# Attention with a spectral feed-forward on one core: the last unit finished 128 rows at a time, the spectral weights folded, loads and a small chain reordered

## The chip, the core and the metric

The kernel runs on one core of a Trainium2 chip. A core has a matrix engine (TensorE, PE in the profile, with PEld for its weight loads), a vector engine (VectorE, DVE), a scalar engine (ScalarE, ACT), GpSimd (POOL), and SyncE (SP), which here only starts transfers. Each engine takes its own instructions strictly in the order in which they were written and waits for others by semaphores; transfers (DMA) are started from the queues of SP, ACT and POOL. Matrix products land in the PSUM memory; everything else lies in SBUF. The metric is the device time of one execution in microseconds (us).

## The reference

The input x is 2 sequences of 2048 rows of 256 numbers, all float32.

```python
xn = layernorm(x)                       # over the 256 columns
q = rope((xn @ wq).reshape(B, S, 16, 16))
k = rope((xn @ wk).reshape(B, S, 4, 16)); v = (xn @ wv).reshape(B, S, 4, 16)
# head i of q uses head i % 4 of k and v
scores = einsum('bshd,bthd->bhst', q, k) / sqrt(16), causal
attn = softmax(scores) @ v, reshaped to (B, S, 256), @ wo
w = complex(w_freq_real, w_freq_imag)   # 256 x 256
ffn = real(ifft(fft(xn) @ w)) + bias    # over the columns
out = x + attn + ffn
```

Since the spectral part is linear in xn, it is one 256 x 256 real matrix (`mff`), made once: inverse-transform table times weights times transform table, with the cosine table `dc` and the sine table `ds` as inputs. The rest is `xn @ mff`.

## The kernel before, in words

**Blocks, units, steps.** The rows are cut into 8 blocks of 512: block n is sequence n % 2, part j = n // 2 of 4. A unit is a block and one of 4 groups of 4 heads; there are 32, in the order of the blocks. A unit takes 4(j+1) steps t, one for each 128 keys, so the first two blocks have 4 steps per unit and the last two 16. The last four steps of a unit lie on the causal diagonal: of the block's 512 columns only those from `lo` on are worked on (512, 384, 256, 128 columns).

**Preparing a block** (`chain`, `project`). `load_x` brings the 512 rows (L170). `row_stats` takes mean and variance of four 128-row pieces on DVE (L237, L238); `row_power` makes the reciprocal root on POOL (L243, L244); `row_shift` makes minus mean times it on DVE (L249); `norm` applies both to the four pieces (L399; DVE for block 0, POOL for the others). PE transposes the block (`transpose_x`, L411), ACT copies it out (`xnT`, L414), and `features` multiplies it with the ordered projection weights `wp` in three parts, K and V together, Q0 and Q1 (tile `ps_q`, products of the helper at L155); ACT copies each out (L427). `rotate` and `split` apply the rotary table and cut each float32 into three bfloat16 parts (seven elementwise passes for each of the three parts, L518 to L556, DVE for block 0 and POOL for the others). SP's queue then stacks the parts into the operands `kst` and `qst` (L393; for most units over a detour through DRAM, `run`).

**A unit.** `maxima` computes rows by keys on PE (tile `sm`, L155, L627, L631) and their maxima on DVE (L636); the negated maxima go through PE, ACT and a transfer (`spread`, L671 to L678) into `qst`, so that `scores` (tiles `st`, then `sp` once all maxima are done; L155, L734, L738) comes out shifted. ACT takes the exponential (L745, L747) and on the diagonal POOL zeroes the upper triangle (`affine_select`, L752). `values` multiplies with the values and a column of ones into `av` (L780), which over all steps of the unit is one accumulation; `take` copies it to SBUF on ACT (L791). For most units the sums of the ones column are divided out over a DRAM detour from POOL's queue (`put` to `scale`). The last two units go another way: `divide` transposes `avs` on PE (tile `ps_a`, L850), divides on DVE (L854, L855), and `turn_back` transposes the result back (tile `ps_t`, L865) for ACT to copy (L869). `output` multiplies with `mff` and `wo_sb` (tile `po`) and adds the residual on DVE (L906); a transfer of 256 rows writes two pieces out (L914). For the last block three of the four terms of `output` are done ahead.

**The spectral matrix** (`spectral_matrix`, once). ACT negates the sine table (L320). Four pieces `left` (tile `ps_ff`) make the two 256 x 256 halves `at_` and `et_` from real and imaginary weights, each as 8 products of 128 x 128 by 128 x 256; two pieces `right` (tile `ps_mff`) make `mff` from them with 8 more each. A `product` is four matmul instructions of 32 columns of weights; on float32 each shows as two entries in the profile, so that a group of 16 matmul entries is two products. The inputs are loaded by six transfers on POOL's queue (`load_late`, L225 to L228).

**What sets the order.** The text of the kernel is a planner: `clock` holds an estimated time for each engine, `there` when a thing will be ready, `use` and `send` advance them by a duration written in the code (0.53 us for `row_stats`, for example). A loop picks the next piece for PE among row maxima (A), scores (B), values (V), spreads (S) and the queues of other pieces (`streams`, each with a step from which it may and one by which it should be done), and emits pieces of the other engines as their estimated start comes up. Each engine then runs in the emitted order. A changed cost or a changed piece therefore shifts the order of all later work. At the start, 48 transposes of the identity (L968) keep PE busy until data is there. PSUM gives three banks to `st`, shared by all small pieces, two pairs to `sm`/`sp` and one to `av`.

Of the kernel before, what the change touches and what calls it, by code (L numbers as in the profile page):

```python
# [23 lines left out]
def tile_attn_plus_spectral_ffn(  # L24
# [141 lines left out]
    def load_x(n):  # L166
        send("sp", 512, [slot("xt")], [("xt", "in", n)])
        take_slot("xt")
        xt[n] = work.tile([P, NI, D], F32, tag="xt", bufs=2, name=f"xt{n}")
        nc.sync.dma_start(out=xt[n], in_=block_rows(n))  # L170
# [46 lines left out]
    def load_late():  # L217

        for name, src, tag, bufs in (
# [6 lines left out]
            send("pool", 256, (), ["spec"])  # L226
        nc.gpsimd.dma_start(out=wo_sb, in_=wo.rearrange("(c p) n -> p c n", p=P))
# [5 lines left out]
    def row_stats(n, i):  # L233
# [5 lines left out]
        use("dve", 0.53, [("xt", "in", n)], [("mv", n)])  # L239
# [7 lines left out]
    def row_shift(n):  # L247
        shift[n] = work.tile([P, NI], F32, tag="sh", bufs=2, name=f"sh{n}")
        nc.vector.scalar_tensor_tensor(  # L249
            shift[n], mv[n][:, :, 0], -1.0, rstd[n], ALU.mult, ALU.mult  # L250
        )
        use("dve", 0.2, [("rs", n)], [("sh", n)])
# [23 lines left out]
    def rotary_table(j):  # L276
        ex = []

        def expand():
# [17 lines left out]
            use("dve", 1.15, at, [("trx", j)])  # L297
# [14 lines left out]

    mff = const.tile([P, NK, D], F32, name="mff")

    def spectral_matrix():
        wre, wim, dc, ds_ = (spec[k] for k in ("wre", "wim", "dc", "ds"))
        neg_s = work.tile([P, NK, D], F32, tag="xr", bufs=3, name="neg_s")
        at_ = work.tile([P, NK, D], F32, tag="xr", bufs=3, name="at_")
        et_ = work.tile([P, NK, D], F32, tag="xr", bufs=3, name="et_")
        nc.scalar.mul(neg_s, ds_, -1.0)  # L320
        use("act", 0.48, ["spec"], ["neg_s"])
# [3 lines left out]
        pieces = []  # L325

        def left(o, name, dst, parts):
            cols = slice(o * P, (o + 1) * P)
            ps = bank(f"ps_ff{o}")[:, :D]
            for a, (w, f) in enumerate(parts):  # L330
                for c in range(NK):
                    product(
                        ps, w[:, c, cols], f[:, c, :],
                        start=(a == 0 and c == 0), stop=(a == 1 and c == NK - 1),
                    )
            nc.scalar.mul(dst[:, o, :], ps, 1.0 / D)
            through_bank(1.87, ["neg_s"], "act", 0.29, [("left", o, name)])

        def right(r):
            cols = slice(r * P, (r + 1) * P)  # L340
            ps = bank(f"ps_mff{r}")[:, :D]
            for a, (w, f) in enumerate(((at_, dc), (et_, neg_s))):
                for c in range(NK):
                    product(
                        ps, w[:, c, cols], f[:, c, :],
                        start=(a == 0 and c == 0), stop=(a == 1 and c == NK - 1),
                    )
            nc.scalar.copy(mff[:, r, :], ps)
            lefts = [("left", o, name) for o in range(NK) for name in ("at", "et")]
            through_bank(1.87, lefts, "act", 0.29, [("mff", r)])  # L350
            if r == NK - 1:
                for tag, k in (
                    ("inv", 0), ("inv", 1), ("attT", 0), ("avs", 0),
# [3 lines left out]

        for o in range(NK):
            pieces.append((["neg_s"], lambda o=o: left(o, "at", at_, ((wre, dc), (wim, ds_)))))
            pieces.append((["neg_s"], lambda o=o: left(o, "et", et_, ((wim, dc), (wre, neg_s)))))  # L360
        lefts = [("left", o, name) for o in range(NK) for name in ("at", "et")]
        for r in range(NK):
            pieces.append((lefts, lambda r=r: right(r)))
        return pieces
# [14 lines left out]
    def project(n):  # L379
# [5 lines left out]
        raw, sw, swp, part, ra, at = {}, {}, {}, {}, {}, {}  # L385
# [710 lines left out]
    while True:  # L1096
# [88 lines left out]
        elif kind == "V":  # L1185
# [3 lines left out]
            if first[u + 1] == v_next:  # L1189
                take(u)  # L1190
# [64 lines left out]
```

## Time and profile before

| | us |
|---|---|
| median of 4 runs | 923.95 (923.50 to 924.41) |
| the profiled execution, its own time | 924.41 |
| its span in the trace | 922.7 |
| PE busy in the span | 902.9 |
| DVE busy | 748.3 |
| ACT busy | 653.9 |
| POOL busy | 371.0 |

The profiled execution is the slowest of the four runs; 1.7 us of its time lie outside the span. Busy time is the union of an engine's instructions. Lines Lnnn are those of the kernel before. In a group or a timeline, `out<-in` names the tiles, `xN` counts instructions, and the remark in brackets tells how long the engine had been idle before and what it waited for.

### The profile page before, as it was taken

What the parts mean: (1) busy time and instruction counts of PE and PEld (TensorE: products, weight loads), DVE (VectorE), ACT (ScalarE), POOL (GpSimd) and SP (SyncE); (2) the same over time, 40 slices, a digit from 0 to 9 for tenths busy, and PEclk for the clock granted to TensorE, in tenths of its full rate; (3) what the DMA queues carried; (4) which work ended last, traced back from release to release, by engine and by line L of the source; (5) the groups of instructions that cost most, each with busy time, mean ns of one, the idle gap of its engine ahead of it and who ended that gap; (6) DMA issues with size and microseconds to landing.
All of it is one profiled execution on the core that took longest, in us unless ns stands there. A gap on an engine that the chain in (4) does not pass through costs nothing.

```text
span 922.7 us, 38985 instructions
## 1 busy us (share of the span) xinstructions
PE 902.9 (98%) x17324; PEld 498.7 (54%) x17324; DVE 748.3 (81%) x1056; ACT 653.9 (71%) x1375; POOL 371.0 (40%) x556
## 2 busy tenths in 40 slices
PE   7999899999999999999999999999999999999997
PEld 4666565555555555555554555555455554645443
DVE  6878887789789996998995999979789988798601
ACT  3266666588657884888866778857687877588784
POOL 7298766835662424822336420302572021102111
PEclk9999999999999999999999999999999999999999
DMA  5435823340244011340002600010143001100000
GB/s 166 119 89 140 211 91 107 112 116 31 75 124 112 27 38 38 107 129 26 15 26 85 152 27 13 27 60 14 34 111 84 14 3 38 49 14 16 25 1 24
DMA packets 41992, 62.13 MB, mean 67 GB/s; under 512 B 8840, under 2 KB 32120, under 8 KB 41824
## 3 DMA queue, kind: packets, MB, share of 16 engines
q1 hardware_dynamic: 32400, 41.18, 16.6%
q0 software_dynamic: 8128, 17.69, 5.8%
q8 instruction: 135, 2.21, 1.0%
q10 hardware_dynamic: 1296, 0.79, 0.3%
q14 instruction: 33, 0.27, 0.1%
HBM read 32.75 MB, written 18.40 MB: 55 GB/s over the span
## 4 chain that ended last, share of the span: by engine, by line
PE 90%; DVE 5%; ACT 3%; issue 1%; DMA 1%; ACTq 0%; POOL 0%; DVEq 0%; POOLq 0%
PE av L780 24%; PE st L155 22%; PE sm L155 17%; PE sm L631 7%; PE po L155 6%; PE ps_q L155 4%; DVE mx L636 2%; PE sm L627 2%; PE sp L155 2%; PE st L738 2%; ACT es L745 1%; PE ps_x L411 1%; ACT es L747 1%; PE st L734 1%; PE ps_m L671 0%
## 5 line engine op out<-in xcount | busy, mean ns | idle before, releaser
L636 DVE TENSOR_REDUCE mx<-sm 128x2 f32<-128x1024 f32 (+3 forms) x640 | 649.2, 1058 | 85.4 <-PE sm L631 41.5
L745 ACT ACTIVATE es<-st 128x512 f32<-128x512 f32 (+3 forms) x1194 | 552.3, 541 | 177.1 <-PE st L155 146.2
L155 PE MATMUL st<-qst,kst 115*32 115x512 bf16 (+3 forms) x4264 | 327.0, 354 | 1.1 <-ACT es L745 0.4
L780 PE MATMUL av<-es,va 128*32 128x512 f32 (+3 forms) x2560 | 299.9, 529 | 0.6 <-issue 0.3
L155 PE MATMUL sm<-kst,qst 112*32 112x512 bf16 x3072 | 239.5, 379 | 0.8 <-issue 0.7
L155 PEld LDWEIGHTS <-kst 115*32 115x32 bf16 x4608 | 160.9, 95 | 140.6 <-issue 65.0
L752 POOL TENSOR_SCALAR_AFFINE_SELECT es<-es 128x256 f32<-128x256 f32 x192 | 77.1, 409 | 273.7 <-ACT es L745 232.5
L155 PEld LDWEIGHTS <-qst 112*32 112x32 bf16 x3072 | 95.9, 96 | 94.3 <-issue 65.5
L631 PE MATMUL sm<-kst,qst 112*32 112x32 bf16 (+15 forms) x2048 | 121.1, 279 | 0.7 <-DMA qst<-part 0.7
L780 PEld LDWEIGHTS av<-es,va 128*32 128x32 f32 x2560 | 85.3, 109 | 28.5 <-issue 2.4
L627 PE MATMUL sm<-mask,ident_h 128*32 128x64 bf16 (+3 forms) x2048 | 99.4, 200 | 1.1 <-DVE mx L636 0.9
L631 PEld LDWEIGHTS <-qst 112*32 112x32 bf16 x2048 | 65.5, 97 | 34.0 <-issue 20.6
L627 PEld LDWEIGHTS <-ident_h 128*32 128x32 bf16 x2048 | 65.3, 95 | 32.1 <-issue 25.0
L906 DVE TENSOR_TENSOR xr<-po,xr 128x256 f32<-128x256 f32 x36 | 15.3, 424 | 51.5 <-PE po L155 49.5
L803 POOL DMA_DIRECT2D res<-avs x30 | 18.2, 608 | 77.1 <-ACT avs L791 75.0
L155 PE MATMUL ps_q<-xnT,wp 128*32 128x512 f32 x384 | 45.2, 599 | 0.0
L747 ACT ACTIVATE es<-sp 128x1024 f32<-128x1024 f32 (+3 forms) x43 | 36.6, 907 | 7.6 <-PE sp L155 7.4
L427 ACT COPY raw<-ps_q 128x512 f32<-128x512 f32 x24 | 14.1, 586 | 34.8 <-PE ps_q L155 34.8
L518 POOL TENSOR_TENSOR ra<-raw,cs 128x512 f32<-128x512 f32 (+1 forms) x21 | 27.3, 1301 | 24.2 <-ACT raw L427 23.0
L738 PE MATMUL st<-qst,kst 115*32 115x480 bf16 (+15 forms) x512 | 36.3, 279 | 0.6 <-issue 0.6
L155 PE MATMUL po<-wo_sb,attT 128*32 128x256 f32 x512 | 34.4, 379 | 0.7 <-ACT attT L869 0.7
L155 PE MATMUL po<-mff,xnT 128*32 128x256 f32 x512 | 34.4, 380 | 0.0
(108 smaller groups left out, 656.7 us busy)
## 6 DMA issues: line engine op xcount, KB each, us to landing
qst<-run SPq DMA_DIRECT2D x62, 128.0 KB
res<-avs POOLq DMA_DIRECT2D x30, 256.0 KB, 3.1
run<-part SPq DMA_DIRECT2D x31, 192.0 KB
qst<-run SPq DMA_DIRECT2D x31, 192.0 KB
xt<-in_L_attn_x_dram SPq DMA_DIRECT2D x8, 512.0 KB
xr<-in_L_attn_x_dram SPq DMA_DIRECT2D x16, 256.0 KB
out_dram<-xr SPq DMA_DIRECT2D x16, 256.0 KB
sw<-raw SPq DMA_DIRECT2D x60, 64.0 KB
```

The source lines that it names most:

```text
L155: nc.tensor.matmul(to[q : q + QD], lhsT[:, q : q + QD], rhs, start=start, stop=stop)
L518: e.tensor_tensor(ra[c][:r], raw[c][:r], cs[j][:r, 0, :], ALU.mult)
L627: nc.tensor.matmul(to[:, at:wd], ident_h[:, q : q + QD], mask[:, q:], start=True, stop=True, skip_group_check=True,)
L631: nc.tensor.matmul(to[:, : at + QD], rows[:, q : q + QD], keys[:, : at + QD], start=False, stop=True, skip_group_check=True,)
L636: nc.vector.tensor_reduce(t["mx"][:, i, 2 * pr : 2 * pr + 2, k], ps[0][:, :, :wd], AX.X, ALU.max)
L738: nc.tensor.matmul(to[:, at:], keys[:, q : q + QD], rows[:, at:], start=False, stop=True, skip_group_check=True,)
L745: nc.scalar.activation(es[u, t, pr][:, e, lo:], ps[:, lo:], AF.Exp, scale=SCALE)
L747: nc.scalar.activation(es[u, t, pr][:, :, lo:], wide[pr][:, :, lo:], AF.Exp, scale=SCALE)
L752: nc.gpsimd.affine_select(out=es[u, t, pr][:, :, lo : lo + P], in_=es[u, t, pr][:, :, lo : lo + P], pattern=[[0, 2], [1, P]], compare_op=A ...
L780: nc.tensor.matmul(av[u][QD * h : QD * (h + 1), lo:], va[at_block[b, t // NI]][:, t % NI, h, :], es[u, t, h // 2][:, h % 2, lo:], start=(t ...
L803: nc.gpsimd.dma_start(out=res[n, c][f], in_=avs[u])
L906: nc.vector.tensor_tensor(xr[n, r][:, e, :], po, xr[n, r][:, e, :], ALU.add)
```

## The change

- **Last unit by 128 rows.** For the very last unit, each diagonal step of `values` closes the 128 columns that need no later keys. `take_part` copies those 128 columns alone, `divide_part` and `turn_back` work on 128 rows, the last term of `output` for a piece needs only its own rows, and the last block's rows go out in four transfers of 128 rows in place of two of 256.
- **Spectral weights folded.** Cosine and sine are even and odd under k to 256 - k. Six small GpSimd instructions add and subtract mirrored columns of the weights into `vc` and `vs`; then one half `left` is needed in place of two, and `right` needs one product per 128 columns of contraction in place of two. The pieces on PE are `left(o, 0)`, `left(o, 1)` for o = 0, 1 and `right(0)`, `right(1)`. A further table `half_sb` is loaded by two transfers on POOL's queue, into one of the eight `es` slots. The negation on ACT is gone.
- **Projections in two pieces.** `features(c, k)` is planned for each half of the contraction, the first as soon as the first half of `xnT` is there; other work may come between them.
- **First loads and table.** Block 0 is loaded by four transfers of 128 rows; statistics of a piece wait for its own piece. The first rotary table's expansion on DVE stands before `row_shift(0)`, not after it.
- **Negative shift on GpSimd.** For blocks 1 to 7 `row_shift` is two POOL instructions in place of one on DVE.
- **Planner costs.** `row_stats` 0.6 for 0.53, the table 1.6 for 1.15.

```diff
 def load_x(n):
-        send("sp", 512, [slot("xt")], [("xt", "in", n)])
+        at = slot("xt")
         take_slot("xt")
...
-        nc.sync.dma_start(out=xt[n], in_=block_rows(n))
+        step = NI if n else 1
+        for i in range(0, NI, step):
+            send("sp", 128 * step, [at], [("xt", "in", n, k) for k in range(i, i + step)])
+            nc.sync.dma_start(out=xt[n][:, i : i + step, :], in_=block_rows(n)[:, i : i + step, :])
...
+        half_sb = spec["half"] = work.tile([P, D], F32, tag="es", bufs=ES, name="half_sb")
+        nc.gpsimd.dma_start(out=half_sb[0:1], in_=dft[0, P : P + 1, :])
+        nc.gpsimd.dma_start(out=half_sb[1:P], in_=dft[1, 1:P, :])
...
     def row_shift(n):
+        if n == 0:
             nc.vector.scalar_tensor_tensor(
                 shift[n], mv[n][:, :, 0], -1.0, rstd[n], ALU.mult, ALU.mult
             )
+        else:
+            nc.gpsimd.tensor_scalar(shift[n], mv[n][:, :, 0], -1.0, None, ALU.mult)
+            nc.gpsimd.tensor_tensor(shift[n], shift[n], rstd[n], ALU.mult)
+            use("pool", 0.4, [("rs", n)], [("sh", n)])
...
-            use("dve", 1.15, at, [("trx", j)])
+            use("dve", 1.6, at, [("trx", j)])
...
+        fold(of_c, up, wre[:, :, up], wre[:, :, down], ALU.add)
+        fold(of_s, up, wim[:, :, up], wim[:, :, down], ALU.add)
+        fold(of_c, far, wim[:, :, down], wim[:, :, up], ALU.subtract)
+        fold(of_s, far, wre[:, :, up], wre[:, :, down], ALU.subtract, True)
+
+        def left(o, a):
+            v, f = ((of_c, dc), (of_s, ds_))[a]
+            if a == 0:
+                held[o] = bank(f"ps_ff{o}")[:, :D], take_slot("st")
+            ps, k = held[o]
+            for c in range(NK):
+                product(
+                    ps, v[:, c, o * P : (o + 1) * P], f[:, c, :],
+                    start=(a == 0 and c == 0), stop=(a == 1 and c == NK - 1),
+                )
...
-            for a, (w, f) in enumerate(((at_, dc), (et_, neg_s))):
-                for c in range(NK):
-                    product(
-                        ps, w[:, c, cols], f[:, c, :],
-                        start=(a == 0 and c == 0), stop=(a == 1 and c == NK - 1),
-                    )
+            for c, f in enumerate((dc[:, 0, :], half_sb)):
+                product(
+                    ps, left_sb[:, c, r * P : (r + 1) * P], f,
+                    start=(c == 0), stop=(c == NK - 1),
+                )
...
-        def features(c):
+        def features(c, k):
+            if k == 0:
+                held[c] = bank(f"ps_q{n}_{c}"), take_slot("st")
+            ps, at_st = held[c]
+            product(ps, wp[:, k, c, :], xnT[n][:, k, :], start=(k == 0), stop=(k == NK - 1))
...
+        if last and t >= j * NI:
+            take_part(u, t - j * NI)
+    def take_part(u, i):
...
+        cols = slice(i * P, (i + 1) * P)
+        nc.scalar.copy(avs[u][:, cols], av[u][:, cols])
+    def divide_part(u, i):
...
+        nc.tensor.transpose(ps, avs[u][:, i * P : (i + 1) * P], ident)
+        nc.vector.reciprocal(rc, heads[:, :, DH])
+        nc.vector.tensor_tensor(
+            att[n][:, i, g - 2], heads[:, :, 0:DH],
+            rc.unsqueeze(2).to_broadcast([P, NKV, DH]), ALU.mult,
+        )
+    def turn_back(n, c, i):
+        ps = bank(f"ps_t{n}_{c}_{i}")[:, 0:P]
+        nc.tensor.transpose(ps, att[n][:, i].rearrange("p g h e -> p (g h e)"), ident)
+        nc.scalar.copy(attT[n][:, c, i * P : (i + 1) * P], ps)
...
+        if terms[-1] == 2 * NK - 1 and n == NB - 1:
+            nc.sync.dma_start(out=out[b, at : at + P, :], in_=xr[n, r][:, e, :])
...
     row_power(0)
     load_late()
+    table_0 = rotary_table(0)
+    table_0[0]()
     row_shift(0)
```

## The prediction

> **What bounds the kernel now.** I read the engines' busy times first, then PE in stretches of the span, then the chain at both ends.
>
> ```profile
> PE 902.9 (98%) x17324; PEld 498.7 (54%) x17324; DVE 748.3 (81%) x1056; ACT 653.9 (71%) x1375; POOL 371.0 (40%) x556
> ...
> 10.00:15.00 5.00, 4.59 (x24) 2.73 (x28) 4.43 (x16) 2.25 (x4) 4.94 (x9) 0.66 0.75 247
> ...
> 100.00:120.00 20.00, 16.80 (x533) 11.84 (x529) 15.45 (x28) 13.96 (x38) 15.52 (x23) 1.00 0.74 194
> 120.00:140.00 20.00, 19.88 (x532) 14.45 (x528) 19.10 (x36) 9.77 (x28) 12.07 (x20) 1.00 0.27 87
> ...
> 220.00:230.00 10.00, 9.37 (x199) 5.51 (x197) 9.79 (x21) 6.85 (x18) 7.77 (x15) 1.00 0.02 5
> ...
> 910.00:915.00 5.00, 3.92 (x60) 1.79 (x53) 0.26 (x1) 2.44 (x5) 2.01 (x5) 1.00 0.00 0
> 915.00:920.00 5.00, 2.59 (x36) 1.35 (x36) 2.12 (x5) 0.59 (x1) 0.00 (x0) 1.00 0.13 43
> ```
>
> A stretch's columns are its length, the busy time of PE, PEld, DVE, ACT and POOL, PE's granted clock, the transfers' share and GB/s. PE is busy for all but 19.8 us. By the same view these lie so: 5.6 up to 34 us, 4.5 from 34 to 140 (3.2 of them in the row from 100 to 120), 2.9 from 140 to 880, 0.6 to 900, 6.2 after 910. So work taken from PE counts in full in the middle; at the start and the end the chain counts.
>
> The start, as the timeline shows it (start, length, engine, line):
>
> ```profile
> 7.83 1.05 POOL L244 TENSOR_TENSOR rs<-rs,neg_half 128x4 f32<-128x4 f32 x1
> 8.92 0.16 DVE L249 SCALAR_TENSOR_TENSOR sh<-mv,rs 128x4 f32<-128x4 f32 x1 [1.51 <-POOL rs L244]
> 9.00 1.63 DVE L293 TENSOR_REDUCE trx<-trig 128x128 f32<-128x128 f32 x8
> 10.54 1.90 DVE L399 TENSOR_SCALAR xt<-xt,rs,sh 128x256 f32<-128x256 f32 x4
> ...
> 26.05 1.05 PE L155 MATMUL ps_ff<-dc,wim 128*32 128x256 f32 x16
> 26.91 1.05 PE L155 MATMUL ps_ff<-neg_s,wre 128*32 128x256 f32 x16
> ...
> 33.08 0.23 POOL L243 TENSOR_SCALAR rs<-mv 128x4 f32<-128x4 f32 x1 [10.16 <-DVE mv L238]
> ```
>
> DVE stands 1.51 us before the shift and expands the table only then; two groups of spectral products start 0.86 us apart; POOL idles 10.16 us. The end, by the chain of waits:
>
> ```profile
> 913.39 0.59 ACT avs L791
> 914.03 0.67 PE ps_a L850 x4
> 914.72 0.27 DVE rc L854
> 915.01 0.43 DVE att L855
> 915.49 0.67 PE ps_t L865 x4
> 916.18 0.59 ACT attT L869
> 916.82 0.68 PE po L155 x8
> 918.83 0.42 DVE xr L906
> ```
>
> After the last `values` (913.37) seven links in a row take 5.9 us; the last two writes take the remaining 3.45.
>
> **Spectral products.** Before: four `left` and two `right`, 12 groups at 0.86 us, 10.3 us of PE. After: 12 products, 6 groups, 5.2 us. PE does 5.2 us less. The negation on ACT (0.63 us) and two copies (0.385 each) go, all beside other work: nothing.
>
> **Folds.** Four POOL instructions of 128 x 254 and two of 128 x 4. No row shows a mirrored read. From below, POOL's 128x256 select, 0.41; from above, a whole 128x512 float32 subtraction, 1.17. I take half of that, 0.6, since the four 128x256 norms take 0.55 each: 2.6 us with the two small ones (range 1.8 to 5).
>
> **First loads.** SP issues four transfers (0.44 to 0.5 us each), so the table's issue moves from 1.30 to about 2.8 and block 1's from 1.83 to 3.3. The whole block landed at 5.16; its last quarter, issued at 2.3, should do so at about 5.1. DVE is in its memsets until 4.64, then takes 2.14 us of statistics without a wait: done 6.8, not 7.32. The table expands there (6.8 to 8.45) while POOL makes the root (1.4 us, as now). If the table lands late, the shift queued behind it waits too; all early loads were over by 7.6, so that costs at most 0.8. Norms begin at 8.7, not 10.54. PE's first transposes follow its warm-up (ended 8.36) at once, where it now idles 1.9 us.
>
> The two-piece projection lets K's first half start after the first copy (11.5) and the second follow the next copy. Its last product ends at about 13.2, against 16.2.
>
> **The clock.** The granted clock was 1.00 in the windows up to 11 us and 0.50 from 12 to 14, after PE's gap from 8.36 to 10.30; the eight transposes took 2.32 us against 1.02 later, K's projection 2.38 against 1.9. I put that loss at 1.8 us. The first gap goes, but a new one comes, next paragraph. I take 1.7 us lost again; ends 0 and 3.4.
>
> **What PE waits for next.** In the emitted order, PE after block 0's last swap product comes to block 1's transposes, K projection and half a `left` before unit 0's first row maximum; the seven other spectral groups that filled this time before are gone or later. Block 1's norms hang on POOL's queue: root 8.3; eight transfer issues (six took 4.45 us, so 5.7 with the two of `half_sb`) to 14.0; ones for block 2 and 1 (2.5 each) to 19.0; root 1.4; ones again 2.6, to 23.1; shift 0.4 (0.24 and 0.15, the rows of L243 and L249); norms 2.2 to 26.1; folds to 28.8. PE is through with block 0 at about 21.8. It then idles about 4 us, does 3.6 us of work and reaches the row maxima at 29.6, or 31.5 at half clock. Their operand landed at 31.8; DVE's chain in front starts 2.9 us earlier, so it is there at 28.9. Idle PE time up to there: 1.4, 0.8 among the norms, three waits for copies at 0.7, 3.9, in all 8.2 for 5.6: plus 2.6.
>
> The Trainium skill speaks against the change here ("TensorE: Matmul & The Clock Gate", Part 1): about 3.4 us of idling put PE at half clock until a busy window has passed. This trace lost the clock after a gap of 1.9 us for about 3.4 us. By the page the new gap costs up to 1.7 us, and without it the sum would be 1.7 better.
>
> **Early stalls.** POOL's rotation of block 1 began at 44.32 and, with block 2's, kept it almost without a pause to 106. Block 1's root and shift had waited for DVE's queue until 33; in the new order both precede, and POOL's rotation starts right after the folds, near 30. So stacks for blocks 1 and 2 come some ten us sooner, and the stalls from 70 to 120, where few scores were left to do while block 2 was made, have less cause. POOL has 2.6 of folds, 1.2 of issues and 0.4 per block more, and DVE is 19.10 of 20 busy in the next stretch. I take 2.0 of the 4.5 us; ends minus 4.0 and plus 2.
>
> **Shift in the middle.** Once (226.09) DVE stood 1.13 us in L249 against 0.15 otherwise, in a stretch where DVE is full and PE idles 0.63. I take 0.5 (0 to 1). Elsewhere POOL's second small instruction replaces a handover.
>
> **The tail.** Scores and the last selects come as before, but two copies of 128 columns (0.28, as the 128x128 exponential) stand before the last exponentials on ACT: plus 0.6. PE meets each part's chain in between; its order has the last `values` after two transposes and an output term: plus 0.2. So the last `values` ends at 914.1. Then, by 128 columns: copy 0.28, transpose 0.27, division 0.3 (a quarter of the columns of L854 and L855, 0.26 and 0.42), two residuals and an output term on the same queues 0.9, transpose 0.27, copy 0.28, output 0.45, residual 0.42: 3.1 us, to 917.2, against 919.25. Four issues at 0.62 on SP fit, and the last write carries 128 KB where two of 256 KB overlapped: 0.5 less. Tail: minus 2.6 (1.0 to 3.3).
>
> **Planner.** Everything later is reordered a little; from 140 to 880 PE idles 2.9 us. I take zero, ends plus and minus 1.5.
>
> **Sum.** -5.2 + 2.6 + 0 (clock, 1.7 for 1.8) - 2.0 - 0.5 - 2.6 + 0 = -7.7, so 924.4 becomes 916.7. The profiled execution is 0.45 above the median; against the median I say 916.3.
>
> **The rivals.**
> - R1, the early stalls stay (DVE at 19.1 of 20 sets them, not POOL) and the clock costs 1.7 more: -7.7 + 2.0 + 1.7 = -4.0, 920. For it: DVE's stretch after 120.
> - R2, the stalls all but go and the new gap is 2 us shorter, POOL's queue being through sooner than I sum it: -9.7 with one of these, -11.7 with both, 914.2 or 912.3; I say 913. For it: POOL's long pause before 44.
> - R3, slower: POOL becomes the bound before 120 us. The folds and issues stand in front of block 1's rotation; if mirrored reads are slow or its projection comes late, block 2's operands land 7 us after today's and PE idles that much more: -5.2 + 2.6 - 0.5 - 2.6 + 7 = +1.3, 925. It decides from a delay of 6 us on. Against it: POOL would need to lose the 14 us by which its rotation starts earlier, and that again.
> - R4, the trimmed products only open waits (the new gap, the tail's interleaving): within 0.2%, 923.5.
>
> **Chances and range.** Forecast 0.50 (914.8 to 918.5), R1 0.20, R2 0.18, R3 0.07, R4 0.05. 0.2% (1.85 us) is about what a measurement tells apart. Faster (below 922.1): the first three but for 0.01, 0.87; same R4, 0.05; slower R3 and that 0.01, 0.08. The range reaches over R2 and R1: 911.5 to 921.5.
>
> **What would show it.** Six spectral groups at 0.86; norms at 8.7, K's product over by 13.3; a PE gap near 22 to 26 with a clock below 1.00 after it; row maxima at 29 to 32; POOL's rotation near 30; under 3 us idle from 34 to 140; the last residual ending 4.3 us after the last exponential, where it is 6.9 now (912.34 to 919.25). Wrong it would be if folds took over 1.2 us each, if PE idled more than now from 34 to 140, or if PE's busy time fell by less than 4.

## The result, and the profile after

The changed kernel takes 927.89 us (median of 52 runs), the kernel before 926.17 us (79 runs, measured beside it and beside the experiments): a ratio of 1.002, with a 95% interval from 1.0013 to 1.0028. It is 0.2% slower. The forecast was 916.3 us with a range from 911.5 to 921.5, 0.8% faster than the 923.95 us then known; it was wrong, in size and in sign. The profiled execution of the changed kernel took 927.19 us, 2.8 more than the one of before, with a span of 925.4 us for 922.7.

The engines' busy times of the changed kernel:

```profile
PE 902.1 (97%) x17228; PEld 494.7 (53%) x17228; DVE 750.0 (81%) x1055; ACT 653.3 (71%) x1378; POOL 381.6 (41%) x578
```

Six groups of spectral products are gone from PE, 5.2 us, but its busy time fell by only 0.8, and its idle time grew by 3.5. The same view by stretches as in the prediction (length, busy time of PE, PEld, DVE, ACT, POOL, PE's granted clock, transfers):

```profile
20.00:25.00 5.00, 2.30 (x20) 0.29 (x12) 4.72 (x9) 0.59 (x1) 4.73 (x8) 0.93 0.31 103
25.00:30.00 5.00, 2.80 (x12) 1.59 (x16) 4.83 (x6) 0.60 (x2) 4.95 (x9) 0.50 0.37 96
30.00:34.00 4.00, 4.00 (x24) 1.07 (x28) 1.63 (x7) 0.94 (x2) 1.99 (x3) 0.50 0.79 212
...
100.00:120.00 20.00, 17.22 (x552) 11.91 (x552) 15.81 (x32) 12.93 (x35) 18.13 (x25) 1.00 0.78 202
120.00:140.00 20.00, 18.66 (x503) 11.54 (x496) 17.81 (x32) 11.75 (x33) 10.50 (x18) 1.00 0.26 80
220.00:230.00 10.00, 9.80 (x204) 5.31 (x196) 9.56 (x24) 8.78 (x20) 5.92 (x12) 1.00 0.14 47
```

PE now idles 8.1 us up to 34 us (5.6 before), 6.2 from 34 to 140 (4.5 before) and 2.6 from 140 to 880 (2.9 before). And from 25 to 34 us it works at half its clock, which makes the work there longer: 1.7 us on block 1's first projection, 1.7 on block 1's transposes (2.74 us for the 1.06 of block 0's) and 0.6 on a spectral group. Another 1.4 us of the busy time are the warm-up at the start, which took 8.30 us in this execution and 6.94 in that of before. That is where most of the 5.2 us went, and more.

The start, as the timeline shows it (start, length, engine, line; lines are those of the changed kernel, in which the norm is L436, the shift L264, a fold L347, the last split pass L595, the row maximum on DVE L676). Below, "the first scores" are unit 0's first products of `maxima` on PE (tile `sm`), and "the first row maximum" is what DVE makes of them:

```profile
7.31 1.64 DVE L307 TENSOR_REDUCE trx<-trig 128x128 f32<-128x128 f32 x8 [0.41 <-DMA trig<-rope_dram]
8.87 0.15 DVE L259 SCALAR_TENSOR_TENSOR sh<-mv,rs 128x4 f32<-128x4 f32 x1
9.05 1.46 DVE L436 TENSOR_SCALAR xt<-xt,rs,sh 128x256 f32<-128x256 f32 x4
...
25.38 3.19 POOL L436 TENSOR_SCALAR xt<-xt,rs,sh 128x256 f32<-128x256 f32 x4
25.98 0.47 PE L448 MATMUL ps_x<-ident,xt 128*128 128x128 f32 x1 [2.98 <-POOL xt L436]
28.88 1.24 DVE L595 TENSOR_TENSOR part<-rb,part 128x512 bf16<-128x512 f32 x1
29.88 3.64 PE L155 MATMUL ps_q<-xnT,wp 128*32 128x512 f32 x16
31.27 0.72 POOL L347 TENSOR_TENSOR vs<-wre 128x254 f32<-128x254 f32 x1
33.30 1.68 PE L155 MATMUL ps_ff<-dc,vc 128*32 128x256 f32 x16
35.21 0.76 DVE L676 TENSOR_REDUCE mx<-sm 128x2 f32<-128x256 f32 x2 [3.47 <-PE sm L671]
```

The opening itself came nearly as told: norms at 9.05, not 10.54 (8.7 told), and block 0's first projection over at 13.72, not 16.1 (13.2 told). But the reader can follow how the lead is lost. PE is done with block 0 at 23.0 and stands 2.98 us before block 1's first transpose, until POOL has normed a piece. It comes out of that gap at half clock, so the projection takes 3.64 us (1.9 at full clock) and a spectral group 1.68 (1.05). DVE has block 0's last split at 30.12, but the first scores stand behind all this on PE's queue. DVE's first row maximum starts at 35.21; before, it was 32.83.

The end, by the chain of waits:

```profile
917.11 0.36 PE av L822 x8
917.46 0.43 PE po L155 x8
917.89 0.28 PE ps_a L919
918.18 0.12 PE ps_t L931
...
918.32 0.28 ACT attT L932
...
919.90 0.68 PE po L155 x8
...
920.60 0.42 DVE xr L971
```

From the last `values` to the last residual it takes 3.55 us (5.9 before), but the last `values` comes 1.9 us after the last exponential (915.58) where it was 1.0 before: on PE it stands behind the transposes and output terms of the other parts.

### The profile page after: what moved, and what is told of

Same layout as the page of the kernel before. It is cut to its first block, busy times and chain, and to the rows that moved or that the text cites. A ratio compares the mean times of both kernels' runs of the same rounds, so it can differ in the third digit from the quotient of the medians.

```text
span 925.4 us, 38869 instructions
## 1 busy us (share of the span) xinstructions
PE 902.1 (97%) x17228; PEld 494.7 (53%) x17228; DVE 750.0 (81%) x1055; ACT 653.3 (71%) x1378; POOL 381.6 (41%) x578
## 3 DMA queue, kind: packets, MB, share of 16 engines
q1 hardware_dynamic: 32480, 41.18, 16.8%
## 4 chain that ended last, share of the span: by engine, by line
PE 88%; ACT 4%; POOL 4%; DMA 2%; issue 2%; DVE 1%; ACTq 0%; SPq 0%; POOLq 0%
PE av L822 24%; PE st L155 23%; PE sm L155 18%; PE po L155 6%; PE sm L671 6%; PE ps_q L155 4%; ACT es L785 3%; PE sp L155 2%; PE sm L667 2%; PE ps_x L448 1%; POOL kst L413 1%; DMA inv<-sums 1%; ACT es L787 1%; PE st L778 1%; DMA xr<-in_L_attn_x_dram 1%
## 5 line engine op out<-in xcount | busy, mean ns | idle before, releaser
L676 DVE TENSOR_REDUCE mx<-sm 128x2 f32<-128x1024 f32 (+3 forms) x640 | 649.8, 1059 | 91.5 <-PE sm L671 43.0
L155 PE MATMUL st<-qst,kst 115*32 115x512 bf16 (+3 forms) x4264 | 331.0, 354 | 1.6 <-ACT es L785 0.7
L671 PE MATMUL sm<-kst,qst 112*32 112x128 bf16 (+15 forms) x2048 | 120.2, 279 | 1.6 <-issue 1.6
L155 PE MATMUL ps_q<-xnT,wp 128*32 128x512 f32 x384 | 50.1, 613 | 0.3 <-ACT xnT L451 0.3
L778 PE MATMUL st<-qst,kst 115*32 115x64 bf16 (+15 forms) x512 | 35.3, 279 | 1.3 <-DMA qst<-mt 0.7
L557 POOL TENSOR_TENSOR ra<-raw,cs 128x512 f32<-128x512 f32 (+1 forms) x21 | 26.9, 1279 | 20.3 <-ACT raw L466 19.4
L155 PE MATMUL po<-mff,xnT 128*32 128x256 f32 x512 | 34.8, 379 | 0.0
```

The source lines that it names most:

```text
L155: nc.tensor.matmul(to[q : q + QD], lhsT[:, q : q + QD], rhs, start=start, stop=stop)
L557: e.tensor_tensor(ra[c][:r], raw[c][:r], cs[j][:r, 0, :], ALU.mult)
L671: nc.tensor.matmul(to[:, : at + QD], rows[:, q : q + QD], keys[:, : at + QD], start=False, stop=True, skip_group_check=True,)
L676: nc.vector.tensor_reduce(t["mx"][:, i, 2 * pr : 2 * pr + 2, k], ps[0][:, :, :wd], AX.X, ALU.max)
L778: nc.tensor.matmul(to[:, at:], keys[:, q : q + QD], rows[:, at:], start=False, stop=True, skip_group_check=True,)
```

## The experiments

Every run is compared with the kernel before on the same chip; ratios are to it, with their 95% intervals. In the runs that take parts of the change away or put them in, each part stands behind a switch that can touch several places; the cuts show the main one in its shortest form. One execution's trace can differ by some 2 us from the next: in the run of the tail alone, whose code is the same up to the last unit, block 2's last split ended at 108.6 us where the profile of before has 106.7, and the offset of 2.1 us was there by 130 us and stayed. So the verdicts rest on the ratios, and the traces tell where to look.

### The gap's clock, and the shift put back

Two runs on the changed kernel. The first puts the shift back on DVE; the second fills PE's new gap with useless work.

```diff
-        if n == 0:
+        if True:
             nc.vector.scalar_tensor_tensor(
                 shift[n], mv[n][:, :, 0], -1.0, rstd[n], ALU.mult, ALU.mult
```

> The changed kernel with the negative shift of blocks 1 to 7 back on DVE, all else kept. Theory A (the shift on GpSimd let the planner put block 1's transposes and projection ahead of unit 0's row maxima on PE, where they wait for POOL, and the idle time halves the clock): without it PE's order has no block 1 work before the first row maximum, that maximum starts near 30 us instead of 34.8, the granted clock stays near 1.00 from 25 to 34 us, and the time is 2.5 to 4 us below the changed kernel, a ratio to before of 0.998 or less. Rival B (the folded products themselves wait for the folds on POOL, so PE idles as long wherever the shift stands): the first row maximum still starts after 33 us, the clock still drops, ratio 1.000 or more.

```diff
         def transpose_x(c):
...
+            if n == 1 and c == 0:
+                fill = ps_av.tile([P, SB], F32, tag="av", name="fill")
+                for _ in range(38):
+                    nc.tensor.transpose(fill[:, 0:P], ident, ident)
```

> The changed kernel with 38 transposes of the identity put on PE in front of block 1's first transpose, into the idle accumulator's bank: 4.9 us of work without use that keeps PE busy during the gap. It separates the clock from the gap. Theory A1 (half clock costs): the clock stays at 1.00, block 1's K projection takes 1.9 us instead of 3.64, the half spectral product 0.9 to 1.05 instead of 1.68, unit 0's first row maximum starts near 32 us instead of 34.8, and the time is 2 to 3 us below the changed kernel (ratio to before near 0.9995). Rival A2 (only the wait for POOL counts; the slow work is made up later): first row maximum 32 us, but the time stays within 0.7 us of the changed kernel, ratio 1.002.

The fill gave 1.0002 [0.9987, 1.0017], 1.7 us less than the changed kernel: the clock stayed at 1.00, the projection took 1.92 us and the first scores came at 32.1 instead of 34.8. The stretch from 20 to 34 us, in the columns of the view by stretches above, first in the changed kernel and then with the fill:

```profile
20.00:34.00 14.00, 9.10 (x52) 2.94 (x48) 11.19 (x20) 2.12 (x4) 11.67 (x19) 0.66 0.47 132
20.00:34.00 14.00, 12.04 (x146) 7.20 (x138) 12.34 (x24) 2.69 (x5) 12.84 (x20) 1.00 0.45 127
```

So useless work on PE made the kernel faster. The shift back on DVE did not: 1.0037 [1.0022, 1.0052]. Its first scores came early (30.57), as its theory had it, but PE there waited 2.92 us for a fold, and the clock was 0.50 from 26 to 28 us. Unit 1 was done 4.4 us before that of the kernel before; the run then lost more from 80 to 140 us, where PE idled 10 us. The shift alone was not to blame for the changed kernel's time; the parts depend on each other.

### Two parts alone

The kernel before with the last unit's 128-row pieces and nothing else of the change, and the kernel before with the fold (six groups for twelve) and nothing else:

```diff
+        last = u == len(units) - 1
+        if last and t >= j * NI:
+            take_part(u, t - j * NI)
...
+        if terms[-1] == 2 * NK - 1 and n == NB - 1:
+            nc.sync.dma_start(out=out[b, at : at + P, :], in_=xr[n, r][:, e, :])
```

> The kernel before with only the last unit finished by 128 rows. Prediction's step: minus 2.6 us, ratio 0.997. Theory C (from the changed kernel's trace): the last residual ends 1.4 us earlier counted from the last exponential, but two copies delay that exponential by 0.3 and the end of the program after the last transfer is 1.5 us longer, so the time is within 0.8 us of before, ratio 0.999 to 1.001. Rival: the tail is slower by itself, over 1.001.

```diff
-    spectral_pieces = stream([("act", ["spec"], [], spectral)], -1, 8)
+    folds, products = spectral_matrix()
+    stream([("pool", ["spec"], [], fold) for fold in folds], -1, 4)
+    stream([("pe", *piece) for piece in products], -1, 8)
```

> The kernel before with only the folded spectral weights. If PE's work taken away counts in full: minus 5.2 us, ratio 0.9944. Theory A: six groups go, but PE used the twelve to fill its wait for unit 0's operands (landing 31.8 us); in the opening the products wait for the folds, so before the first row maximum nothing is gained, and at most the two right pieces' 3.4 minus 0.9 us stand after it: minus 1 to minus 3 us, ratio 0.997 to 0.999. Rival B (the folds are a cost by themselves): first row maximum later than 32.2 us, clock below 1.00, ratio 1.000 or more.

The tail alone: 0.9982 [0.9964, 1.0000], so 1.7 us faster, between the two expectations, with an interval that just reaches nothing. The fold alone: 1.0130 [1.0103, 1.0157], 12 us slower, with 5.2 us less of PE's work in it. There the planner laid the work out so that POOL's norm of a block waited 11.96 us for DVE's shift and block 1's rotation began at 58.1 us, not 44.3. This says that the fold's order can cost much, not yet what the products themselves are worth.

### What PE's and POOL's time is worth near 70 us

Both in the kernel before: useless transposes on PE, and useless memsets on POOL.

```diff
             nc.scalar.copy(va[n][:, :, :, 0:DH], pv.rearrange("p i (h d) -> p i h d", d=DH))
+            if n == 2:
+                for _ in range(26):
+                    nc.tensor.transpose(ps[:, 3 * P : 4 * P], ident, ident)
```

> Before, with 26 useless transposes on PE (about 0.115 us each by the fill of the earlier run, 3.0 us) behind block 2's V transposes, near 70 us; no operand of block 2's K comes later by it, those of its Q have 10 us in hand on POOL. Theory A: PE is the bound there (its rows show 99% busy between 60 and 80 us), the end comes 2.5 to 3.0 us later, ratio 1.0027 to 1.0033. Theory B: under half of it reaches the end, 0 to 1.5 us, ratio 1.000 to 1.0016, and PE's idle between 80 and 140 us falls by the rest.

```diff
                 ra[c] = work.tile([P, SB], F32, tag=f"ra{min(n, 1)}", bufs=1, name=f"ra{n}_{c}")
+                if n == 2 and c == NK:
+                    for _ in range(6):
+                        e.memset(ra[c], 0.0)
```

> Before, with six useless memsets of 128x512 on POOL (0.53 us each, 3.2 us) in front of block 2's first rotation, near 72 us. Theory A: block 2's operands have slack, as PE is the bound: 0 to 1 us, ratio 1.000 to 1.001. Theory B: the chain passes the delay on to the end, 2 to 3.2 us, ratio 1.002 to 1.0035, block 2's last split ends about 3 us later (106.7 before) and PE's idle between 80 and 140 us grows by it.

3.1 us more of PE: 1.0034 [1.0019, 1.0050], 3.1 us, in full. 3.45 us more of POOL: 0.9997 [0.9979, 1.0016], nothing. My rival that POOL's chain for block 2 passes every delay on fell. POOL's timeline tells why; first with the memsets on POOL:

```profile
71.20 3.45 POOL L520 MEMSET ra<- 128x512 f32 x6
...
82.28 0.58 POOL L806 DMA_DIRECT2D res<-avs  x1 [1.09 <-ACT es L748]
84.14 1.29 POOL L521 TENSOR_TENSOR ra<-raw,cs 128x512 f32<-128x512 f32 x1
```

and then with the transposes on PE:

```profile
71.09 1.29 POOL L521 TENSOR_TENSOR ra<-raw,cs 64x512 f32<-64x512 f32 x1
84.73 0.58 POOL L806 DMA_DIRECT2D res<-avs  x1 [5.19 <-ACT es L748]
86.60 1.28 POOL L521 TENSOR_TENSOR ra<-raw,cs 128x512 f32<-128x512 f32 x1
```

The third line is block 2's next rotation; before, it began at 83.96 (at 44 us both these executions were 0.7 to 0.9 us ahead of that one). On POOL's queue it stands behind `put` of unit 1, which needs that unit's `avs`, and so PE. Memsets are taken out of POOL's waits up to there; PE's work makes the wait longer. So near 70 us PE sets the time, directly and through POOL.

### What the spectral products are worth where they stood

The first run leaves every second spectral product out of the kernel before, with no fold and the same order of all else. Its time is the disputed term alone.

```diff
-            for a, (w, f) in enumerate(parts):
+            for a, (w, f) in enumerate(parts[:1]):
...
-            for a, (w, f) in enumerate(((at_, dc), (et_, neg_s))):
+            for a, (w, f) in enumerate(((at_, dc),)):
```

> Before, in its own order, with every second product of the spectral matrices left out (six groups of 0.86 us stay of twelve; the spectral matrix is thereby wrong). Nothing is folded and POOL does nothing more, so this is the disputed 5.2 us of PE by itself. Theory A (they count in full): 5.2 us faster, ratio 0.9944. Theory C (in before DVE's rotations and splits of block 0 run without a gap from 16.8 to 30.8 us and the first scores wait for their last operand over DMA; the eight left groups run on PE from 23.5 to 31.2 us in their shade, and only the four right groups, between the scores, are on the path): the four left groups taken away leave a hole of 3.4 us in front of the first scores and the first row maximum stays within 0.5 us of 32.8 us; at most the 1.7 us of the two right groups come, less what a colder clock costs: ratio 0.998 to 1.001.

1.0020 [1.0005, 1.0034]. Half of the products away, and the kernel is 1.9 us slower. What stood above them in the kernel before is seen in its timeline:

```profile
30.08 0.69 DVE L556 TENSOR_TENSOR part<-rb,part 128x512 bf16<-128x512 f32 x1
32.16 0.18 PE L631 MATMUL sm<-kst,qst 112*32 112x32 bf16 x1 [0.71 <-DMA qst<-part]
32.73 0.18 DVE L238 BATCH_NORM_AGGREGATE mv<-bn 128x2 f32<-128x6 f32 x1
32.83 0.72 DVE L636 TENSOR_REDUCE mx<-sm 128x2 f32<-128x256 f32 x2
```

and in that of the run without half of them:

```profile
31.18 0.18 PE L631 MATMUL sm<-kst,qst 112*32 112x32 bf16 x1 [3.00 <-DMA qst<-part]
31.50 1.38 PE L155 MATMUL ps_mff<-dc,at__326 128*32 128x256 f32 x15
32.98 0.18 DVE L238 BATCH_NORM_AGGREGATE mv<-bn 128x2 f32<-128x6 f32 x1
33.08 0.72 DVE L636 TENSOR_REDUCE mx<-sm 128x2 f32<-128x256 f32 x2
34.44 1.60 PE L155 MATMUL ps_mff<-dc,at__326 128*32 128x256 f32 x16
```

DVE rotates and splits block 0 almost without a pause from 16.8 to 30.8 us and then takes the statistics of a later block to 32.9; the first row maximum follows on its queue without a wait. The first scores on PE wait for a transfer of this chain's parts; the eight left groups run on PE meanwhile. Without half of them PE waits 3.00 us instead of 0.71 for such a transfer. The scores then come a microsecond sooner, at 31.18 for 32.16, and still the first row maximum is at 33.08 for 32.83: it stands behind DVE's own work, which in this execution was 0.26 us later from the last split on. After the gap the clock was down: 0.53 from 32 to 34 us and 0.61 from 34 to 36, so that the right groups took 1.38 and 1.60 instead of 1.07 to 1.13. Over these four us that is some 1.7 us of PE's work (my estimate from the two clocks), as much as the two missing right groups saved.

The same with the hole filled:

```diff
             nc.scalar.mul(dst[:, o, :], ps, 1.0 / D)
+            if o == NK - 1 and name == "et":
+                for _ in range(26):
+                    nc.tensor.transpose(whole[:, D : D + P], ident, ident)
```

> The kernel of before with half of the spectral products left out (the spectral matrix is thereby wrong), and 26 useless transposes (0.115 us each, 3.0 us) in the hole between the last left group at 28 us and the first scores at 31.5 us. Theory C (shade, and the hole's clock): the clock stays at 1.00 from 20 to 60 us, the first row maximum stays at 32.8 to 33.1 us, the 1.7 us of the two right groups now come, ratio 0.9975 to 0.999, that is 2 to 4 us under the same kernel with the hole (1.002). Rival E (the 5.2 us were lost elsewhere, in the preparation of block 2): the ratio stays at 1.001 to 1.003.

1.0009 [0.9989, 1.0028]: between the two expectations, and its interval reaches into both. The first row maximum was again at 33.09 us, so three kernels with 6.9, 3.4 and 6.5 us of this work on PE ahead of the scores have it within 0.3 us. But the 1.7 us of the right groups did not clearly come, and the clock fell to 0.93 between 34 and 60 us in this execution all the same. How much of the 1.9 us the clock alone makes is not settled.

### The other products and the shift, apart from each other

In the changed kernel, with the old products back:

```diff
-    folds, products = spectral_matrix()
-    stream([("pool", ["spec"], [], fold) for fold in folds], -1, 4)
-    stream([("pe", *piece) for piece in products], -1, 8)
+    spectral_pieces = stream([("act", ["spec"], [], spectral)], -1, 8)
```

> The changed kernel with the spectral products of before (twelve groups on PE, no folds on POOL), all else as changed. Theory A (PE's work counts in full, the fold is worth its 5.2 us): 927.2 + 5.2 = 932 or so in a profile, ratio to before 1.006 to 1.009. Theory B (in the first 120 us the chain that prepares blocks 1 and 2 over POOL's queue sets the end, and PE's work is partly cover for it): the twelve groups fill the gap while POOL's norms run, the clock stays up, and the time is at or below that of the changed kernel: ratio 0.995 to 1.002.

with the old products and the shift on DVE as well:

```diff
-    folds, products = spectral_matrix()
...
+    spectral_pieces = stream([("act", ["spec"], [], spectral)], -1, 8)
...
-        if n == 0:
+        if True:
             nc.vector.scalar_tensor_tensor(
```

> The changed kernel with the spectral products of before and the negative shift back on DVE; the tail, the pieces of the projection, the loads, the table's order and the costs stay changed. Theory A: as the run without the fold alone, ratio 1.006 to 1.009, as the 5.2 us of PE's work are back. Theory B: the opening is 2.5 us earlier up to the K product, nothing new is put in front of block 1's norms, and the tail's 1.5 to 2 us come: ratio 0.994 to 0.999.

and this one with half of its products left out, by the edit shown above for before:

```diff
-            for a, (w, f) in enumerate(parts):
+            for a, (w, f) in enumerate(parts[:1]):
```

> The kernel without fold and without the shift on POOL, with every second spectral product left out (the spectral matrix is thereby wrong). Its DVE chain of block 0 ends at 28.3 us and its scores began at 28.2 to 29.1 us behind the last left group. Theory A: 5.2 us under that kernel, ratio to before 0.989 to 0.990. Theory C: 0 to 1.7 us under it, ratio 0.993 to 0.997, its first row maximum still at 30 to 30.5 us.

| ratio to before | shift on POOL | shift on DVE |
|---|---|---|
| folded | 1.0020 [1.0013, 1.0028] (the change) | 1.0037 [1.0022, 1.0052] |
| not folded | 1.0020 [1.0004, 1.0036] | **0.9950 [0.9932, 0.9969]** |
| not folded, half of the products left out | not run | 0.9964 [0.9950, 0.9978] |

The kernel with neither (no fold, shift on DVE) takes 920.89 us; it is faster than the kernel before and than the change. Beside it, 5.2 us less of PE's work is worth nothing again (1.3 us slower, with intervals that overlap); there too the clock fell, to 0.50 from 30 to 36 us, so this run does not part the shade of DVE's chain from the clock. And in the first column the fold with its six groups less is worth nothing either. Its DVE timeline beside that of its halved brother, first with all products:

```profile
27.62 0.69 DVE L667 TENSOR_TENSOR part<-rb,part 128x512 bf16<-128x512 f32 x1
30.36 0.72 DVE L751 TENSOR_REDUCE mx<-sm 128x2 f32<-128x256 f32 x2
```

and with half of them:

```profile
27.59 0.69 DVE L667 TENSOR_TENSOR part<-rb,part 128x512 bf16<-128x512 f32 x1
30.34 0.72 DVE L751 TENSOR_REDUCE mx<-sm 128x2 f32<-128x256 f32 x2
```

DVE's chain is 2.5 us earlier than before, which the loads and the table bring, and the first row maximum with it, whatever PE has in between. In the changed kernel with the old products (shift on POOL), PE's timeline shows what the shift does to it:

```profile
25.17 0.33 PE L505 MATMUL ps_x<-ident,xt 128*128 128x128 f32 x1 [0.64 <-POOL xt L493]
26.14 0.38 PE L505 MATMUL ps_x<-ident,xt 128*128 128x128 f32 x1 [0.64 <-POOL xt L493]
...
27.93 2.77 PE L157 MATMUL ps_q<-xnT,wp 128*32 128x512 f32 x16
```

Block 1's transposes and projection come ahead of the first scores, one piece at a time at POOL's pace, and the clock is 0.88 from 20 to 34 us. Unit 1 is done 5.1 us later than with the shift on DVE.

### The order of the first scores

In the changed kernel, and in that without the fold, one number of the planner is altered, so that the first scores come sooner on PE's queue:

```diff
-        MULT, SUB, CAST, NORM = (0.72, 0.72, 0.46, 0.33) if n == 0 else (1.23, 1.13, 0.63, 0.53)
+        MULT, SUB, CAST, NORM = (0.72, 0.72, 0.46, 0.33) if n == 0 else (1.23, 1.13, 0.63, 1.6)
```

> The changed kernel with one number of the planner's costs altered (one norm on POOL put at 1.6 us, not 0.53), by which the first 32 scores stand ahead of block 1's transposes and of the fold products on PE's queue. Theory C (the changed kernel lost what its opening gained because the first scores stand on PE behind block 1's transposes, which wait for POOL's norms, and behind a fold product): the first row maximum comes at 30 to 31.5 us instead of 35.2, unit 1 is done 2 to 4 us earlier than in the changed kernel, ratio 0.995 to 1.000. Rival D (the POOL queue of block 2 sets the end whatever the opening does): the ratio stays at 1.001 to 1.004.

> The changed kernel without the fold, shift on POOL, with one number of the planner's costs altered (one norm on POOL put at 1.6 us, not 0.53): all eight left groups and the first 32 scores now stand ahead of block 1's projection on PE, and six of the eight ahead of its transposes. Theory C (the shift on POOL costs through PE's order alone): the first row maximum comes at 30 to 31.5 us (32.3 or later in the run without fold), the clock stays at 1.00 between 20 and 34 us, ratio 0.995 to 0.999. Rival F (POOL itself, its shift ahead of the norms and the order that the planner then lays out for blocks 1 and 2): ratio 1.000 to 1.004.

With the fold: 1.0041 [1.0025, 1.0056], a miss of my theory. The first row maximum did come at 31.31 us, but PE had 7.3 us of idle time from 20 to 34, with a clock of 0.50 from 26 to 32, and its units 0 and 1 ended as in the kernel before. Without the fold: 0.9992 [0.9975, 1.0010], between what I had put for PE's order alone and for POOL itself. Here the opening was as good as without the shift on POOL (first row maximum 31.18, clock 1.00, unit 0 done 3.5 us before that of the kernel before) and 2.6 us of the 6.5 came back. The rest was lost from 80 to 140 us. A likely place is POOL's queue, in this run:

```profile
93.60 0.52 POOL L958 DMA_DIRECT2D sums<-den  x1 [4.04 <-DVE den L952]
97.24 0.61 POOL L962 DMA_DIRECT2D inv<-sums  x1 [3.12 <-DMA sums<-den]
97.87 1.28 POOL L630 TENSOR_TENSOR ra<-raw,cs 128x512 f32<-128x512 f32 x1
```

Block 2's last rotation stands behind the two waits for a unit's sums and begins at 97.87; it stood ahead of them at 88.01 in the kernel of 0.995, at 92.88 in the kernel before, and behind them, at 102.35, in the folded one with the shift on DVE. No run changed this place alone, so it stays an argument.

What of the fold's 8 us (1.0037 for 0.9950, shift on DVE in both) lies where is told only in part: 1.3 us with the missing products, and 0.8 us at the first row maximum (31.19 for 30.36 us), after PE's 2.92 us of waiting for a fold and DVE's last split, which ended 1.35 us later; some of this may be the same time. The rest, between 80 and 140 us, is open.

### The opening alone

The kernel of 0.995 with the last unit as in before:

```diff
-        last = u == len(units) - 1
+        last = False
```

> Before with the projection's pieces, the loads, the table's order and the costs as changed, without the tail, the fold and the shift on POOL. Theory C: the opening's gain alone, 2.4 to 4 us, ratio 0.9955 to 0.9975, and the difference to the run that had the tail too (0.995) is the tail's price, 1 to 2 us. Rival: the opening's gain is lost again before 140 us, ratio 0.999 to 1.001, and the tail with the order of the later blocks made the 0.995.

0.9972 [0.9956, 0.9988]: 2.6 us from the loads, the table, the projection's pieces and the planner's two costs together. The tail on top gives the 0.995, so 2.0 us, with intervals that overlap.

## Why the prediction was wrong

**The step that failed: "Spectral products", put into the sum as -5.2.** I had written that PE's work counts in full in the middle and that at the start the chain counts, and then counted work at 23 to 36 us in full. Two thirds of it lay in the shade of DVE's chain of block 0: the first row maximum stayed where it was without them. Left out in before's own order the work brought +1.9 us, not -5.2; left out of the fastest kernel, +1.3; and the changed kernel with the old products back takes the same 1.0020. So 5 to 7 of the 9.6 us of error (-7.7 forecast, 1.9 measured by the ratio) lie in this one term. For the third that was not in the shade, the clock that fell in the emptier stretch is the likely reason; it is not settled. The other parts do not simply add up to the rest, as the table shows. Two of the signs that I had named for being wrong came: PE's busy time fell by 0.8, not by 4 or more, and PE idled more than before from 34 to 140 us. I had even listed that the first scores' operand would land at 28.9; the question that I did not ask was what PE would have done until then.

**Opening idle +2.6:** right in its amount, 8.05 us for the 8.2 I told. But the first scores came at 34.80, where I told 29.6, or 31.5 at half clock: PE was through with block 0 at 23.0 (21.8 told), POOL's norms ended at 28.57 (26.1 told), and then came the slow work.

**Clock 0:** right in kind. The old loss at 12 to 14 us went (1.00 from 10 to 20 now), and a new one came after the new gap, larger than told: 1.7 us on the projection, 0.6 on a group and 1.7 on the transposes, in front of the first scores. The fill prices it at 1.7 us in the end, the size that I told. The old loss is not in every execution either. In the six other kept runs with before's opening PE stood 0.78 to 1.83 us between its warm-up and its next work; after 1.68 us and more the clock was 0.50 or 0.51 from 12 to 14 us, after 0.78 and 0.93 (the two pads) it stayed at 1.00, and block 0's first projection was over at 15.4, not 16.1. By the rule of the Trainium skill that I had weighed ("TensorE: Matmul & The Clock Gate", Part 1, about 3.4 us of idle time) a gap of 2.98 us was near the limit; here it was enough, as 1.68 us and more were at 10 us, and the clock had begun to fall while PE still stood (0.59 from 24 to 26 us).

**Early stalls -2.0:** wrong in sign, 6.2 us for 4.5. POOL's rotation of block 1 did begin at 34.3 instead of 44.3, ten us sooner. (What stood behind DVE's queue until 33 us in the kernel before was block 1's shift alone; the root at 33.08 is block 2's, block 1's ran at 18.48.) But block 2's began at 72.39 (71.97 before): its projection keeps its planned step on PE, and POOL waited 4.15 us for it. What is early on one queue has to meet the next engine's order.

**Shift in the middle -0.5:** PE's idle from 220 to 230 fell from 0.63 to 0.20 us, as told; at the start the shift on POOL cost 6.5 us without the fold, which I had at nothing.

**Tail -2.6:** the mechanism right, the size off. The last residual came 5.4 us after the last exponential (6.9 before, 4.3 told): the last `values` ended 1.9 us after it, where I told 1.2, since more stood ahead of it on PE than I gave it; the links from there took 3.55 us, 3.1 told. And what follows the last residual grew from 3.45 us to 4.4 (3.9 to 4.3 in the other runs with this tail), where I had told 0.5 less for a smaller write. The runs price the tail at 1.7 and 2.0 us.

**Folds:** 0.64 to 1.17 us each, 0.6 told, and 3.25 for the four. **The rivals:** R3 had the sign and nearly the time (925), but its mechanism is not borne out near 70 us: 3.45 us more on POOL before block 2's rotation were worth nothing in the kernel before, and in the changed one POOL stood there 4.15 us for its input. What POOL costs between 80 and 140 us stays open. R1 was right that the early stalls stay; its clock term of 1.7 us more is in the trace, but not in the price that the fill gives.

## What to carry to other kernels

Before work is taken off the busiest engine, ask of the very stretch where it stands which chain ends last there: 5.2 us of PE's work were worth nothing at 23 to 36 us, two thirds of them under another engine's chain, and 3.1 us were worth 3.1 at 70 us. Work that fills a wait can also keep the clock up, so that taking it away can cost: here useless work in a gap won 1.7 us. And where a planner lays out the order, parts of a change must be tried apart: here two that were to help cost 6.5 us (the shift) and 8 (the fold), each put alone into the kernel without them, which was the fastest.

## What the runs showed of the hardware

DVE's passes take longer beside POOL's. The last seven passes of block 0 (L557 to L595 of the changed kernel) took 4.39 us in the kernel before and in the one of 0.995, where POOL stood idle beside them. They took 5.60 us with the folds beside them (fold, shift on DVE) and 5.94 with norms and folds (the changed kernel: the last pass 1.24 us for 0.69). POOL's norms took 0.80 us each there, 0.54 when alone. Beside POOL's memsets (21.92 to 24.28 us) DVE's passes with two operands in SBUF kept their 0.69; a cast beside another memset (at 21.51 us) took 0.63 for 0.43. "SBUF — State Buffer" of the Trainium skill (section "SBUF: two separate sides") has it that the two share a pair of ports, that one blocks the other for a whole instruction, and that a DVE instruction with two operands in SBUF is concerned only where GpSimd reads SBUF too; these rows of the two-operand passes agree. I had costed the folds and the shift on POOL as lying beside DVE's work for nothing. With the fold alone (shift on DVE) the last split ended 1.35 us later than in the kernel of 0.995, at 29.66 for 28.31. In the changed kernel itself DVE then stood 3.47 us for PE, so that there its longer passes were not what the first row maximum waited for.

A second one: a single stall of 3.33 us near 105 us, in one execution of the halved kernel, brought the clock down to 0.50 in the two us from 108 on, so that the price of a stall is not its length alone.
